# The ending of a fused vision-tower kernel in another order: last residual inside block 30's MLP product, block 29's tiles fed from the weight bank

## The chip, the core and the metric

The kernel runs on one core of one Trainium2 chip. A core has five engines that run their own instruction streams in order and wait for each other through semaphores: TensorE (PE, matrix products into PSUM), VectorE (DVE), ScalarE (ACT), GpSimd (POOL) and SyncE (SP, which here only issues transfers). ACT and POOL issue transfers too. The metric is the device time of one execution in microseconds (us); less is better. The time before is 2111.08 us, the median of three runs (2110.65 to 2120.14).

## The reference

Three stages with float32 throughout, on 16384 tokens of 256 features, in 32 blocks of 512 tokens.

```python
h = tokenizer(x)                       # windowed rfft, then @ W.T
# layer: normalised input, retention, MLP
x0 = layernorm(h)
z  = layernorm(x0) * g1 + b1
q, k, v = z @ Wq.T + bq, z @ Wk.T + bk, z @ Wv.T + bv
mem_t = decay * mem_{t-1} + k_t * v_t  # a scan along the tokens
x1 = x0 + q * mem                      # "residual" of the retention
h  = h + x1 + relu(layernorm(x1) @ W1.T + b1) @ W2.T + b2
# mixture of experts: 8 experts, the 2 best of each token
tok = layernorm(h)
p = softmax(tok @ router_w.T); two best, their shares rescaled to sum to 1
h = h + tok + sum over both of share_e * (gelu(tok @ w1[e] + b1[e]) @ w2[e] + b2[e])
```

## The kernel before

**Blocks.** `vit_tower_kernel` works through blocks 0 to 31 of 512 tokens as a software pipeline. In pass i of its loop (i = 0 to 30) block i, called `new`, is embedded and gets its retention; block i - 1, `mid`, gets its MLP (`mlp_in`, eight products of 128 hidden features each into one of three PSUM tiles called sums, then `mlp_out` in two halves u = 0, 1 of two times eight products); block i - 2, `old`, gets its choice of experts (`logits`, `choose`), the places of its rows (`place`) and its scatter. After the loop comes a hand-written ending (lines 1287 to 1371) for `last` = block 31, `mid` = block 30 and `old` = block 29.

**Tiles of tokens.** A block's tokens are scattered by expert into a buffer in HBM (`xbuf`): eight indirect writes from POOL's queue (`scatter`, line 819), two for each quarter of the block. Whenever enough are there, `take` (lines 858 to 934) makes a table on DVE that says for each new tile of 256 rows which expert it belongs to and where its rows start, and appends the tiles to a list. There are 131 such tiles, 0 to 130 in order; `take(30)` appends four that belong to block 29, `take(31)` eighteen that belong to block 30. Block 31 isn't scattered: its tokens go through all eight experts (`Expert`), with shares from `combine`.

**Steps of a tile.** `advance` runs each stage of the tiles in order, and `expert_halves` (or `expert_step`, the same in one piece) puts one step together. With n the next tile to enter, a step emits:

- *load* of the tiles up to n + 3: from SP's queue the expert's weights (641.5 KB, line 965), the rows transposed into xh (a DMA transpose, line 972) and the rows' shares and numbers into xg (line 975),
- *turn* of tile n + 1: two ACT copies that put xh's halves together into xT (line 995),
- *enter* of tile n: eight PE products into a PSUM tile of pool mm, which has two buffers (line 1002), and two Gelu activations on ACT (line 1010),
- then, in the second half, *leave* of tile n - 1: eight products into pool tm, which has three buffers (line 1019); *sums* of that tile: DVE scales them into y (lines 1031 to 1038), and POOL adds them to the output in HBM with two indirect adding transfers (line 1048); and *fetch* of the tiles up to n + 3.

A tile's two adds wait until the two adds of the tile before have landed, and for the store of the tile's block (`before = added[-2:] + [self.block.stored]`, line 1046), since they read and write the same output rows. y has four buffers, the weights w five, xh six.

**The weight bank.** The embedding's weights and inputs give up their memory once block 31 is embedded, and `load_bank` (line 938) then loads all eight experts' weights into one tile, one 641.5 KB transfer from ACT's queue per `next(weights)`. Tiles of block 30 load no weights of their own: `fetch` (line 982) copies them from the bank, on DVE or ACT by turns (line 989).

**Order.** `manual_schedule` keeps SP's, PE's, DVE's and ACT's instructions in the order in which the program emits them. So the order of the calls in the ending is the order on every engine. POOL's instructions, too, run in one order. `slot_halves` (line 1158) lets the loop run a tile step only while more than `LEFT` = 3 tiles are left.

**The ending.** Block 31 is embedded and a tile step runs; block 30's eight `mlp_in` products follow, with a tile step after the fourth and `last.features1` (eight PE transposes of zz through pool mm, copied to hT by ACT) after the sixth; then block 29's choice, a tile step and its scatter; `retention(0)`, `mlp_out(0)`, `take(30)`, `mlp_out(1)`, `retention(1)`; five tile steps with block 30's `features3` (the same for tok), choice and scatter and block 31's `residual` (transposes of ret on PE, then adds, statistics and normalisation to zz on DVE) among them; `take(31)`; block 31's `features2`, a tile step, `sum_up`, its eight `mlp_in` products with tile steps, and `mlp_out` with tile steps. Last come block 31's choice, and its eight experts among the 12 tiles that are left.

In `choose`, the weight of a token's second expert needs exp. For blocks 0 to 30 POOL raises e to that power (line 769); for block 31 ACT does it (line 767).

Of the kernel before, what the change touches and what calls it, by code (L numbers as in the profile page):

```python
# [36 lines left out]
def vit_tower_kernel(  # L37
# [312 lines left out]
    class Block:  # L350
# [381 lines left out]
        def choose(self):  # L732

            ps = self.lg
            shape = [P, TT, E]

            def wide(a):
                return a.unsqueeze(2).to_broadcast(shape)

            lg = small.tile(shape, F32, name="lg")  # L740
            top = small.tile([P, TT], F32, name="top")
            if self.i == NS:
                first_key = small.tile([P, TT], F32, name="first_key")
            else:
                first_key = self.row.bitcast(F32)[:, :, FIRST]
            turned = small.tile([P, TT, G], F32, name="turned_lg")
            nc.vector.transpose(turned.rearrange("p t g -> p (t g)"), ps.rearrange("p t g -> p (t g)"))
            nc.vector.tensor_reduce(top, turned[:, :, :E], AX.X, ALU.max)
            nc.vector.tensor_tensor(lg, turned[:, :, :E], wide(top), ALU.subtract)
            key = small.tile(shape, F32, name="key")  # L750
            self.oh = oh = small.tile([P, 2, TT, E], F32, name="oh")
            nc.vector.scalar_tensor_tensor(key, lg, 0.0, key0, ALU.is_equal, ALU.mult)
            nc.vector.tensor_reduce(first_key, key, AX.X, ALU.max)
            nc.vector.tensor_tensor(oh[:, 0], key, wide(first_key), ALU.is_equal)
            nc.vector.scalar_tensor_tensor(lg, oh[:, 0], -3.0e38, lg, ALU.mult, ALU.add)
            second = small.tile([P, TT], F32, name="second")
            nc.vector.tensor_reduce(second, lg, AX.X, ALU.max)
            nc.vector.tensor_tensor(key, lg, wide(second), ALU.is_equal)
            nc.vector.tensor_tensor(key, key, key0, ALU.mult)
            nc.vector.tensor_reduce(top, key, AX.X, ALU.max)  # L760
            nc.vector.tensor_tensor(oh[:, 1], key, wide(top), ALU.is_equal)
            dtype = F32 if self.i == NS else BF16
            self.both = small.tile(shape, dtype, name=f"both_{dtype.name}")
            nc.vector.tensor_tensor(self.both, oh[:, 0], oh[:, 1], ALU.add)
            self.ex = small.tile([P, TT], F32, name="ex")
            if self.i == NS:
                nc.scalar.activation(self.ex, second, AF.Exp)
            else:
                nc.gpsimd.tensor_tensor(self.ex, euler, second, ALU.pow)

# [7 lines left out]

        def combine(self):

            diff = small.tile([P, TT], F32, name="diff")
            second = small.tile([P, TT], F32, name="second")
            self.weights(diff, second)
            shape = [P, TT, E]
            self.share = self.both
            nc.vector.tensor_tensor(self.share, self.both, second.unsqueeze(2).to_broadcast(shape), ALU.mult)
            first = self.oh[:, 0]
            nc.vector.tensor_tensor(first, first, diff.unsqueeze(2).to_broadcast(shape), ALU.mult)
            nc.vector.tensor_tensor(self.share, self.share, first, ALU.add)
# [68 lines left out]
    def take(n, block, writes):  # L858
# [40 lines left out]
        expert = small.tile([P, KMAX], F32, name="expert")[:, :k]  # L899
        nc.vector.tensor_reduce(expert, past, AX.X, ALU.add)  # L900
        table = four.tile([P, 2, KMAX], I32, name="table")[:, :, :k]
        if block.i >= NS - 1:
            nc.vector.tensor_scalar(table[:, 0, :], expert, float(E - 1), None, ALU.min)
        else:
            nc.vector.tensor_scalar(table[:, 0, :], expert, float(P), float((E - 1) * P), ALU.mult, ALU.min)
# [47 lines left out]
    class Tile:  # L953
# [6 lines left out]
        def load(self):  # L960
            t = self.t
            self.w = five.tile([P, NW], F32, name="w")
            if self.block.i < NS - 1:
                wrow = nc.sync.value_load(self.table[:, 0, t : t + 1], min_val=0, max_val=(E - 1) * P)
                nc.sync.dma_start(out=self.w, in_=wex[bass.ds(wrow, P), :])

            def rows():
                row = nc.sync.value_load(self.table[:, 1, t : t + 1], min_val=0, max_val=ROWS - S)
                return xbuf[bass.ds(row, S), :]

            self.xh = six.tile([P, 2 * KD, S], U16, name="xh")
            read = nc.sync.dma_start(out=self.xh, in_=rows().bitcast(U16)[:, : 2 * D], transpose=True)
            unordered("rows", read, self.writes)
            self.xg = twelve.tile([P, 2, RW - D], I32, name="xg")
            read = nc.sync.dma_start(out=self.xg, in_=rows()[:, D:].rearrange("(c p) d -> p c d", p=P))
            unordered("rows", read, self.writes)
# [3 lines left out]
            return self.block.put == TT  # L980

        def fetch(self):
            if self.block.i >= NS - 1:

                assert len(loaded) == E
                t = self.t
                engine, copy = ((nc.vector, nc.vector.tensor_copy), (nc.scalar, nc.scalar.copy))[t % 2]
                e = engine.value_load(self.table[:, 0, t : t + 1], min_val=0, max_val=E - 1)
                copy(self.w.unsqueeze(1), bank[0][:, bass.ds(e, 1), :])
# [165 lines left out]

    LEFT = 3

    def slot_halves(known, load=True, sums=True):

        if len(tiles) - at["enter"] > LEFT and at["enter"] + 2 <= known:  # L1160
            yield from expert_halves(load=load, sums=sums)

    def slot(known, load=True):
# [8 lines left out]
    with tc.manual_schedule(engines=MANUAL):  # L1172
# [3 lines left out]
        for i in range(NS):  # L1176
# [54 lines left out]
            if i:  # L1231
                qkv = new.qkv()
                if old:
                    old.logits()
                    old.choose()
                if i >= EARLY:
                    next(ahead)
                next(qkv)
                next(qkv)
                tile_steps = slot_halves(known, sums=False)  # L1240
                next(tile_steps, None)
                next(qkv)
                if old:
                    writes = old.place(at_once=False)
                    old.scatter(1)
                run(tile_steps)
                if old:
                    old.scatter(2, last_product[0])
                next(qkv)
                advance("sums", at["leave"])  # L1250
                later = slot_halves(known, load=False)
                next(later, None)
                next(qkv)
                new.first_norm()
                for m in range(KD):
                    new.scan(m)
                if EARLY <= i < NB - 2:
                    xs[i + 2] = load_x(i + 2)
                mid.mlp_out(0)
                if old:  # L1260
                    old.scatter(3, last_product[0])
            else:
                xs[i + 2] = load_x(i + 2)
                new.first_norm()
                for m in range(KD):
                    new.retention(m)
# [33 lines left out]
        old.join3(nc.vector.tensor_copy)  # L1300
        for m in range(KH):
            mid.mlp_in(m)
            if m in (1, 3, 5, 7):
                next(weights)
            if m == TT - 1:
                expert_step()
            if m == KH - 3:
                last.features1()
        next(weights)
        old.logits()  # L1310
        old.choose()
        expert_step()
        writes = old.place()
        next(weights)
        restore_weights()
        last.first_norm()
        last.retention(0)
        mid.mlp_out(0)
        next(weights)
        take(NS - 1, old, writes)  # L1320
        next(weights)
        mid.mlp_out(1)
        last.retention(1)
        beside = expert_halves(fetch=False)
        next(beside)
        mid.features3()
        mid.rows()
        advance("leave", at["enter"] - 1)
        mid.logits()
        mid.choose()  # L1330
        run(beside)
        expert_step(fetch=False, sums=False)
        writes = mid.place()
        advance("sums", at["leave"])
        expert_step(fetch=False, sums=False)
        last.residual()
        expert_step(fetch=False, sums=False)
        advance("sums", at["leave"])
        expert_step(fetch=False)
        take(NS, mid, writes)  # L1340

        last.features2()
        expert_step(turn=False)
        mid.store()
        last.sum_up()
        for m in range(KH):
            last.mlp_in(m)
            if m == TT - 1:
                advance("turn", at["enter"] + 1)
            if m == KH - 3:  # L1350
                expert_step()
        expert_step()
        last.mlp_out(0, expert_step)
# [107 lines left out]
```

## Time and profile before

| what | us |
|---|---|
| median of three runs | 2111.08 |
| profiled execution | 2116.49 |
| its span, first to last instruction | 2114.7 |
| PE busy | 2077.4 (98%) |
| DVE busy | 1674.8 (79%) |
| ACT busy | 1100.8 (52%) |
| POOL busy | 886.9 (42%) |
| mean granted clock of PE | 0.994 |
| block 30's first `mlp_in` product starts | 1865.10 |
| block 31's residual, transposes start | 1925.04 |
| block 31's first `mlp_in` product starts | 1948.66 |
| block 31's choice: Exp's table load starts | 2007.14 |
| PE's last group of products | 2106.37, for 3.62 |

All starts are counted from the beginning of the span of the profiled execution. In a line of a timeline the columns are the start, the duration of the group, the engine, the line of the kernel, the operation, output and inputs with their shapes, how many, and in brackets the idle time of the engine before it and what ended that. "ACTq" and "SPq" are those engines issuing a transfer. In a line of the windows view come the stretch, its length, then for PE, PE's weight loads, DVE, ACT and POOL the busy time and the number of instructions, the granted clock, the share of the DMA engines' time, and GB/s.

### The profile page before, as it was taken

The page shows a single profiled execution, that of the slowest core. Times are in us where ns is not written, and L with a number is a line of the kernel's source. Part 1 is how long each engine was busy: PE and PEld are TensorE (multiplying, and loading weights), DVE is VectorE, ACT ScalarE, POOL GpSimd, SP SyncE. Part 2 cuts the span into 40 slices and gives each one's busy share as a digit, 9 for nine tenths or more (in the row PEclk, how much of TensorE's full clock was granted, in tenths as well). Part 3 has the DMA queues.
Part 4 walks back from the last instruction along what each step waited for, and adds up shares of the span by engine and source line. Part 5 has one row for each costly group of instructions (what it writes and reads, how often), then busy time and mean ns, then how long its engine had stood idle before and what let it go on. Part 6 is the DMA issues. An engine that isn't in the chain of part 4 may idle for free.

```text
span 2114.7 us, 30454 instructions
## 1 busy us (share of the span) xinstructions
PE 2077.4 (98%) x9042; PEld 1576.0 (75%) x9042; DVE 1674.8 (79%) x5179; ACT 1100.8 (52%) x1966; POOL 886.9 (42%) x768
## 2 busy tenths in 40 slices
PE   8999999999999999999999999999999999998999
PEld 5777677777777777777777777787777787676776
DVE  6778888888888888888888888888888888767445
ACT  2344455655545565554556555455665545543453
POOL 1032234444444444544444444444444444535444
PEclk9999999999999999999999999999999999999999
DMA  4031256766676676567667766766776567688653
GB/s 142 4 123 64 80 131 138 160 143 129 134 157 146 155 160 139 125 143 159 156 143 160 150 122 136 157 156 143 163 157 118 138 149 161 138 197 168 91 69 50
DMA packets 424519, 283.21 MB, mean 134 GB/s; under 512 B 355104, under 2 KB 391072, under 8 KB 420256
## 3 DMA queue, kind: packets, MB, share of 16 engines
q1 hardware_dynamic: 373424, 208.35, 42.5%
q0 software_dynamic: 49632, 67.39, 17.8%
q10 hardware_dynamic: 1296, 5.52, 0.8%
q8 instruction: 71, 1.16, 0.2%
q14 instruction: 96, 0.79, 0.1%
HBM read 118.36 MB, written 86.52 MB: 97 GB/s over the span
## 4 chain that ended last, share of the span: by engine, by line
PE 74%; DVE 11%; ACT 5%; DMA 5%; issue 2%; POOL 2%; SPq 1%; another core or an unknown queue 0%; ACTq 0%; DVEq 0%; POOLq 0%
PE tm L650 17%; PE sums L339 13%; PE tm L396 9%; PE sums L524 9%; PE mm L1002 8%; PE tm L1019 8%; DMA turned<-planes 3%; DVE st L263 2%; PE mm L540 1%; ACT planes L318 1%; ACT tokT L332 1%; PE tm L1098 1%; PE mm L1081 1%; PE mm L539 1%; SPq L326 1%
## 5 line engine op out<-in xcount | busy, mean ns | idle before, releaser
L1048 POOL DMA_INDIRECT out<-y,xg x226 | 369.2, 1634 | 432.7 <-DVE y L1038 220.2
L650 PE MATMUL tm<-w_sb,aT 128*128 128x256 f32 x2048 | 454.7, 380 | 0.0
L339 PE MATMUL sums<-hT,w_sb 128*128 128x512 f32 x1024 | 451.7, 593 | 1.3 <-ACT aT L640 1.3
L650 PEld LDWEIGHTS tm<-w_sb,aT 128*128 128x128 f32 x2048 | 386.7, 190 | 57.2 <-DVE z L611 4.8
L819 POOL DMA_INDIRECT xbuf<-row,to x248 | 257.1, 1037 | 294.3 <-DVE ks L560 170.5
L339 PEld LDWEIGHTS sums<-hT,w_sb 128*128 128x128 f32 x1024 | 193.4, 190 | 219.9 <-issue 201.0
L396 PE MATMUL tm<-wu,xv 128*128 128x256 f32 x1280 | 282.5, 379 | 0.0
L318 ACT COPY planes<-zz 128x1024 uint16<-128x1024 uint16 x100 | 99.3, 1041 | 342.0 <-DVE zz L292 342.0
L396 PEld LDWEIGHTS tm<-wu,xv 128*128 128x128 f32 x1280 | 242.7, 190 | 32.7
L1002 PE MATMUL mm<-xT,w 128*128 128x256 f32 x1048 | 252.5, 384 | 6.9 <-ACT xT L995 3.8
L1019 PE MATMUL tm<-w,ge 128*128 128x256 f32 x1048 | 253.4, 385 | 0.0
L1002 PEld LDWEIGHTS mm<-xT,w 128*128 128x128 f32 x1048 | 201.3, 193 | 49.9 <-issue 16.0
L1019 PEld LDWEIGHTS tm<-w,ge 128*128 128x128 f32 x1048 | 195.9, 191 | 31.4 <-issue 2.9
L640 ACT ACTIVATE aT<-sums,vec 128x512 f32<-128x512 f32 x256 | 167.0, 690 | 60.6 <-PE sums L339 59.3
L995 ACT COPY xT<-xh 128x512 uint16<-128x512 uint16 x262 | 182.1, 767 | 24.4 <-DMA xh<-xbuf 15.4
L283 POOL TENSOR_SCALAR rstd<-mv 128x4 f32<-128x4 f32 x62 | 42.0, 678 | 333.2 <-DVE mv L264 296.7
L1010 ACT ACTIVATE ge<-mm,w 128x256 f32<-128x256 f32 x262 | 109.9, 474 | 137.5 <-PE mm L1002 76.3
L1036 DVE TENSOR_TENSOR y<-tm,w 128x512 f32<-128x512 f32 x131 | 90.6, 691 | 97.9 <-PE tm L1019 86.6
L332 ACT COPY hT<-turned 128x512 uint16<-128x512 uint16 x100 | 66.2, 762 | 80.5 <-DMA turned<-planes 80.5
L263 DVE BATCH_NORM_STATS2 st<-h 128x6 f32<-128x256 f32 x256 | 104.8, 409 | 3.3
L332 ACT COPY tokT<-turned 128x512 uint16<-128x512 uint16 x116 | 76.5, 760 | 58.7 <-DMA turned<-row 58.7
L524 PE MATMUL sums<-hT,wqkv_sb 128*128 128x256 f32 x360 | 107.1, 379 | 0.0
(224 smaller groups left out, 3105.4 us busy)
## 6 DMA issues: line engine op xcount, KB each, us to landing
w<-in_wex SPq DMA_DIRECT2D x113, 641.5 KB
xb<-in_x SPq DMA_DIRECT2D x32, 1040.0 KB
out<-h SPq DMA_DIRECT2D x31, 512.0 KB
bank<-in_wex ACTq DMA_DIRECT2D x8, 641.5 KB
xbuf<-row,to POOLq DMA_INDIRECT x248
out<-y,xg POOLq DMA_INDIRECT x226
xh<-xbuf SPq DMA_TRANSPOSE x131
xg<-xbuf SPq DMA_DIRECT2D x131, 4.0 KB
```

Of the source, the lines that this page charges most:

```text
L263: nc.vector.bn_stats(self.st[:, t, :], src[:, t, :])
L332: copy(to[:, 1 - i], self.turned[:, :, i, k, :])
L339: nc.tensor.matmul(ps, lhsT=w[:, k, ts(m, P)], rhs=rhs[:, k, :], start=k == 0, stop=k == KD - 1)
L396: nc.tensor.matmul(ps[:, n, :], lhsT=xv[:, i, j, :], rhs=wu[:, i, j, :], start=j == 0, stop=j == J - 1)
L524: nc.tensor.matmul(g[:, n, :], lhsT=lhsT, rhs=rhs, start=False, stop=True, skip_group_check=True)
L640: nc.scalar.activation(self.aT[:, m, :], ps, AF.Relu, bias=vec[:, MB1 + m : MB1 + m + 1])
L650: last_product[0] = nc.tensor.matmul(ps[:, i, :], lhsT=self.aT[:, k, ts(u * 2 + i, P)], rhs=w2_sb[:, k, :], start=k == 0, stop=k == KH - 1,)
L819: write = nc.gpsimd.indirect_dma_start(out=xbuf, out_offset=bass.IndirectOffsetOnAxis(ap=self.to[:, c, t : t + 1], axis=0), in_=self.row[: ...
L995: nc.scalar.copy(halves[:, :, :, 1 - i], self.xh[:, i * KD : (i + 1) * KD, :])
L1002: nc.tensor.matmul(ps[:, m, :], lhsT=self.w[:, k * D + m * P : k * D + (m + 1) * P], rhs=self.xT[:, k, :], start=k == 0, stop=k == KD - 1,)
L1019: last_product[0] = nc.tensor.matmul(ps[:, c, :], lhsT=self.ge[:, k, ts(c, P)], rhs=w[:, (2 + k) * D : (3 + k) * D], start=k == 0, stop=k ...
L1048: add = nc.gpsimd.indirect_dma_start(out=out, out_offset=bass.IndirectOffsetOnAxis(ap=number[:, c, :], axis=0), in_=y[:, c, :], in_offset= ...
```

## The change

- The loop lets one tile more enter in pass 30 (`left=LEFT - (i == NS - 1)`), so the ending starts with one tile fewer.
- `load_bank` is driven once after each of block 30's eight products, and no longer later.
- The tile step between block 29's choice and its places is gone; `retention(0)` stands before `place`.
- `retention(1)` stands between the two products of block 30's `mlp_out(0)`, and block 31's `residual` between those of `mlp_out(1)`.
- `take(30)` stands between the two halves u = 0 and u = 1 as before; a tile step and block 31's `features2` follow `mlp_out(1)`.
- Block 31's first `mlp_in` products stand among block 30's `features3`, choice and `place`. Block 30's scatter is split into two parts with a tile step between.
- The tiles of block 29 load no weights; `fetch` copies them from the bank, as for block 30.
- In all, the ending runs one tile step fewer before `take(31)`, 13 tiles instead of 12 are left for the last stretch with block 31's experts, and the loop has run the tile between.
- Block 31's Exp moves from `choose` to `combine`, two tile steps later.

```diff
             if self.i == NS:
-                nc.scalar.activation(self.ex, second, AF.Exp)
+                self.second = second
...
         def combine(self):
 
+            nc.scalar.activation(self.ex, self.second, AF.Exp)
...
-        if block.i >= NS - 1:
+        if block.i >= NS - 2:
             nc.vector.tensor_scalar(table[:, 0, :], expert, float(E - 1), None, ALU.min)
...
-            if self.block.i < NS - 1:
+            if self.block.i < NS - 2:
                 wrow = nc.sync.value_load(self.table[:, 0, t : t + 1], min_val=0, max_val=(E - 1) * P)
                 nc.sync.dma_start(out=self.w, in_=wex[bass.ds(wrow, P), :])
...
         def fetch(self):
-            if self.block.i >= NS - 1:
+            if self.block.i >= NS - 2:
...
-    def slot_halves(known, load=True, sums=True):
-
-        if len(tiles) - at["enter"] > LEFT and at["enter"] + 2 <= known:
+    def slot_halves(known, load=True, sums=True, left=LEFT):
+
+        if len(tiles) - at["enter"] > left and at["enter"] + 2 <= known:
...
-                later = slot_halves(known, load=False)
+                later = slot_halves(known, load=False, left=LEFT - (i == NS - 1))
...
         for m in range(KH):
             mid.mlp_in(m)
-            if m in (1, 3, 5, 7):
+            if m in (0, 1, 2, 3, 4, 5, 6, 7):
                 next(weights)
             if m == TT - 1:
                 expert_step()
             if m == KH - 3:
                 last.features1()
-        next(weights)
         old.logits()
         old.choose()
-        expert_step()
-        writes = old.place()
-        next(weights)
         restore_weights()
         last.first_norm()
         last.retention(0)
-        mid.mlp_out(0)
-        next(weights)
+        writes = old.place()
+        out_steps = mid.mlp_out_steps(0)
+        next(out_steps)
+        last.retention(1)
+        run(out_steps)
         take(NS - 1, old, writes)
-        next(weights)
-        mid.mlp_out(1)
-        last.retention(1)
-        beside = expert_halves(fetch=False)
+        out_steps = mid.mlp_out_steps(1)
+        next(out_steps)
+        last.residual()
+        run(out_steps)
+        expert_step()
+        last.features2()
+        beside = expert_halves()
         next(beside)
+        last.mlp_in(0)
         mid.features3()
         mid.rows()
-        advance("leave", at["enter"] - 1)
+        run(beside)
         mid.logits()
         mid.choose()
-        run(beside)
-        expert_step(fetch=False, sums=False)
-        writes = mid.place()
-        advance("sums", at["leave"])
-        expert_step(fetch=False, sums=False)
-        last.residual()
-        expert_step(fetch=False, sums=False)
-        advance("sums", at["leave"])
-        expert_step(fetch=False)
+        expert_step()
+        writes = mid.place(at_once=False)
+        mid.scatter(2)
+        last.mlp_in(1)
+        expert_step()
+        mid.scatter(TT)
         take(NS, mid, writes)
-
-        last.features2()
-        expert_step(turn=False)
-        mid.store()
-        last.sum_up()
-        for m in range(KH):
+        for m in range(2, KH):
             last.mlp_in(m)
             if m == TT - 1:
+                expert_step(turn=False)
+                mid.store()
+                last.sum_up()
+            if m == KH - 2:
                 advance("turn", at["enter"] + 1)
-            if m == KH - 3:
+            if m == KH - 1:
                 expert_step()
         expert_step()
```

## The prediction

> **What bounds the kernel now.** I read the page first, then the windows, then PE's timeline for its gaps, and last the timelines of POOL, ACT and SP for what runs beside it.
>
> ```profile
> PE 2077.4 (98%) x9042; PEld 1576.0 (75%) x9042; DVE 1674.8 (79%) x5179; ACT 1100.8 (52%) x1966; POOL 886.9 (42%) x768
> ...
> 1865.00:1899.80 34.80, 34.80 (x138) 21.95 (x137) 19.42 (x63) 17.00 (x32) 12.58 (x9) 1.00 1.06 259
> 1899.80:1926.80 27.00, 25.24 (x126) 19.18 (x125) 21.26 (x89) 10.00 (x17) 14.34 (x14) 1.00 0.56 136
> 1926.80:1948.80 22.00, 15.51 (x60) 12.40 (x58) 16.65 (x71) 8.09 (x16) 13.69 (x12) 0.77 1.05 209
> ...
> 2000.40:2015.00 14.60, 10.54 (x58) 8.28 (x57) 9.17 (x35) 8.61 (x14) 7.72 (x6) 0.88 0.47 59
> ```
>
> PE is full everywhere but in two stretches of the ending, around the last residual (1926 to 1949) and the last choice of experts (2000 to 2015), where the granted clock falls too. PE's timeline has the gaps:
>
> ```profile
> 1938.69 1.11 PE L305 MATMUL mm<-ident,zz 128*128 128x128 f32 x4 [3.36 <-issue]
> 1942.23 3.78 PE L1002 MATMUL mm<-xT,w 128*128 128x256 f32 x8 [2.43 <-ACT hT L306]
> 1945.81 3.01 PE L1019 MATMUL tm<-w,ge 128*128 128x256 f32 x8
> ...
> 2009.97 3.44 PE L1002 MATMUL mm<-xT,w 128*128 128x256 f32 x8 [3.76 <-ACT xT L995]
> ```
>
> With 1.04, 0.72, 0.70 and 0.24 us elsewhere from 1865 on, PE idles 12.25 us. Eight products that take 1.89 us at full clock take 3.78, 3.01 and 3.44 after the long gaps, and four transposes 1.11 for 0.60: 5.1 us more. So 17.3 us is all that PE can win. The second gap is the table load for Exp (ACT 2007.14, 1.28 us, L767, then Gelu's, 2009.94, 1.28 us), with the next tile's xT queued behind it.
>
> But PE isn't alone. POOL's timeline of the scatter-adds, two per tile:
>
> ```profile
> 1952.68 1.76 POOL L1048 DMA_INDIRECT out<-y,xg  x1 [3.44 <-DVE w L989]
> 1959.77 1.54 POOL L1048 DMA_INDIRECT out<-y,xg  x1 [3.48 <-DMA out<-y,xg]
> ...
> 2099.55 1.55 POOL L1048 DMA_INDIRECT out<-y,known  x1 [2.99 <-DMA out<-y,known]
> 2101.41 1.54 POOL L1048 DMA_INDIRECT out<-y,known  x1 [0.30 <-issue]
> 2105.96 1.56 POOL L1048 DMA_INDIRECT out<-y,known  x1 [3.01 <-DVE zz L1106]
> 2107.83 1.78 POOL L1048 DMA_INDIRECT out<-y,known  x1 [0.30 <-issue]
> ```
>
> A tile's adds wait until the previous tile's have landed (L1046). The last tile's y is ready at 2101.03 (DVE L1038, 2100.41 + 0.62), yet its first add goes at 2105.96, 6.41 after the first of the pair before it. From tile 106 (1945.84) on every pair starts 6.3 to 7.5 us after the one before, though its y had been ready 3.4 to 17 us: this chain never waits for PE. From tile 108 (1959.77) to 130 it takes 146.2 us for 22 tiles, 6.645 each. PE's last product ends at 2109.99, and what follows (DVE, the store) ends the span at 2114.7; the last add, issued by 2109.61 and landed some 2.2 us later (a 6.4 us interval less 3.45 of issue and 0.8 of restart), is about 2 us ahead of that. Shorten PE alone, and after 2 us the adds set the end.
>
> The profiled execution took 2116.49 us, its span 2114.7. The median is 5.4 below. Between 1936 and 1942 DVE pauses 1.60, 1.30 and 0.77 us between instructions that wait for nothing else, and nowhere else in the trace; tile 106's adds come 8.71 after tile 105's, 2.1 over the usual interval. I take this pause as this execution's own.
>
> **The change, part by part.**
>
> *One tile more in block 30's loop.* 3.45 us of PE (L1002 and L1019, 1.73 each between starts) go before block 31's embedding; they also cover the 0.29 us wait at 1845.28. Everything behind comes 3.16 later, and one step fewer remains. Sum zero, gain 0.3.
>
> *Bank loads after each product; no tile step after the choice.* ACT issues eight 641.5 KB loads at 0.33 to 0.38 us each, inside products of 1.72 us; the issue time is hidden by PE's three sums buffers. Their waits may not be:
>
> ```profile
> 1874.10 1.06 SPq L972 DMA_TRANSPOSE xh<-xbuf  x1
> ...
> 1882.52 0.33 ACTq L944 DMA_DIRECT2D bank<-in_wex  x1
> 1882.89 1.07 ACT L306 COPY hT<-mm 128x512 f32<-128x512 f32 x2 [3.15 <-DMA xh<-xbuf]
> ```
>
> The third load stood until 1882.5 for tile 105's transposed read, issued by SP at 1874.10, 8.4 us earlier, and held the copies behind it. In the new order tile 105's *turn* itself comes into the step at m = 3, since the loop is one tile ahead. SP's chain before that read (planes, rows, store) is only 1.4 us later, so it lands at 1883.9; ACT then needs 1.38 (turn) and 0.84 (Gelu of tile 104) before PE's second features1 transposes may have their PSUM buffer: 1886.15. PE is there at 1882.4. Wait 3.75 us. Lower bound: the quickest read on the chain of waits took 6.39 (1815.45), which leaves 1.7. Upper: two more bank loads ahead, 1.9 each at the 333 GB/s of that stretch: 7.6. After it, the two gaps of 3.36 and 3.76 gave slow products and the one of 2.96 (1824.04) did not, so I add 1.55 (3.44 - 1.89): s = 5.3, between 1.7 and 9.2. [...]
>
> *Retention(1) between the halves of mlp_out(0), residual between those of mlp_out(1).* Call X the end of mlp_out(0), 1899.74 before. Now X = 1899.74 + 3.16 - 3.45 (the step gone) + 5.15 (L339 at 1906.49 to 1911.64) + s = 1904.6 + s = 1909.9. From X, DVE does 1.8 (adds and statistics, L657 to 1901.60), 3.8 (the table, to 1905.37) and 7.5 (residual, 1926.88 to 1934.37): zz at X + 13.1. PE has 3.45 + 0.87 + 3.45 + 3.45 = 11.2. It waits 1.9, and 0.4 for the first hT copy. That is the old 7.5 us wait with fillers, though not filled.
>
> *mlp_in(0) as filler.* DVE's second half of mlp_out(1) (1906.69 to 1912.80, 6.1) gives tok at X + 19.2; PE, with a tile's L1002 and one product, is there at X + 17.5: 1.7 idle.
>
> *place after one step.* DVE now has tile 104's sums (1.7), tile 105's (y after its product, to X + 23.0), the bank copy that replaces a load (0.83 and 0.86 ahead of it, 1951.06) and the choice (2.95): X + 27.7. PE comes at X + 25.5: 2.2 idle. The four weight loads saved are 2.6 MB that nothing waits for; four copies (0.83 DVE, 1.26 ACT) lie beside PE.
>
> *Exp in combine.* 2.8 us on ACT stay, but PE then has an expert's 3.43 us and a tile's 1.73 with filled buffers; I count 0.1, at most 2.8 were that cover gone. The 3.76 and 1.55 go.
>
> PE's sum: 17.6 out, 5.3 + 2.3 + 1.7 + 2.2 + 0.1 = 11.6 in, so 6.0 less. **The adds' sum decides**: tile 104's y comes behind all that DVE work, at X + 21.0 (X + 19.3 + 1.7). Tiles 105 and 106 follow at 6.65 each. Then four row scatters (1.27 each, L819) stand before tile 107's adds and four before tile 108's, each adding 2.4 to an interval (3.45 + 0.3 + 5.1 + 0.2 = 9.0): tile 108 at X + 52.3. Before, tile 104 went at 1922.93 and eight scatters held 105 until 1937.13; tile 108 at 1959.77, or 1957.7 without the pause. Now it is 1956.9 + s = 1962.2. From there the same 22 intervals and the same end run: 4.5 us later than an undisturbed before, 2.4 later than the profiled one. PE's end is over 5 us ahead of that and buys nothing.
>
> Against its own time: 2116.49 + 2.4 - 1.9 (the 2 us by which the adds were not last) = 2117.0. Against the median, which I take as without the pause, 2111.1 + 4.5 = 2115.6. I say 2115. With s at its bounds 2112 and 2119.5. The 22 intervals ranged from 6.34 to 7.47; at 6.38 throughout they save 5.8, at 6.9 they cost 5.6.
> [...]
>
> **Rivals.** (1) *PE still sets the end.* With four loads gone the intervals shrink to 6.38 and the read lands early (s = 1.7): 2115 - 5.8 - 3.6 = 2105.6, and PE's saving of 6 to 11 shows. For: the median and PE's end lay within 2 us. Against: the lag of up to 17 us. Below 2100.5 only if PE also loses its three small waits.
> (2) *ACT stands at a bank load; slower.* The eighth load issued 12.5 us after the seventh (1889.45, 1901.95), when ACT had nothing to do. Now first_norm and ks stand behind it, and PE's retention(1) needs that ks. ACT would issue it at 1891.1 and needs 3.1 after; PE comes at 1900: a wait w costs w - 5.8. At 12.5 that is 6.7: 2121.7. It decides from 12.4. Against: the loads are earlier than the reads that it stood for.
> (3) *Exp's gap only moves.* Up to 2.8 on PE, nothing on the adds: 2115.
>
> **How the numbers follow.** About 0.5% (10.6 us: 2100.5 and 2121.6) can be told from no change. My case 0.55 (2108 to 2121), rival 1 0.22 (2098 to 2108; 0.06 below 2100.5), rival 2 0.15 (2121 to 2130; 0.13 above), rival 3 and the rest 0.08 (0.01 faster, 0.02 slower). Faster 0.07, same 0.78, slower 0.15; range 2102 to 2126.
>
> **What would show it.** PE without the 3.76 us gap at the last choice, and no Exp on ACT there; a new gap of 2 to 7 us before features1's second transposes (L305 from zz) with ACT's xT waiting for xh; gaps near 2 before the last residual's and the tokens' transposes and before L796. Pairs of adds 6.3 to 7.1 apart to the last, which now lags its y by over 8 us, not 4.9; the span's last waits are for adds. I am wrong if the adds' intervals lie under 6.2 or adds wait for y.

## The result, and the profile after

The changed kernel takes 2129.36 us (median of six runs, 2123.84 to 2131.96), the kernel before 2110.86 in the runs beside it: a ratio of 1.0077, with a 95% interval of 1.0054 to 1.0101, so slower by 16 us (the two medians alone lie 18.5 us apart). I had forecast 2115, with a range from 2102 to 2126, and "slower" at 0.15. The profiled execution took 2129.20 us, its span 2127.4.

The page and the windows view of the changed kernel, in the stretches shown of before:

```profile
PE 2078.0 (98%) x9042; PEld 1576.9 (74%) x9042; DVE 1677.8 (79%) x5181; ACT 1102.0 (52%) x1968; POOL 888.3 (42%) x768
...
1865.00:1899.80 34.80, 29.48 (x103) 16.06 (x101) 12.48 (x39) 11.84 (x22) 11.52 (x8) 0.95 1.13 209
1899.80:1926.80 27.00, 19.52 (x70) 13.61 (x70) 15.50 (x53) 4.60 (x8) 8.29 (x8) 0.81 0.63 161
1926.80:1948.80 22.00, 19.04 (x90) 13.61 (x90) 18.35 (x74) 10.95 (x18) 5.50 (x4) 0.92 0.39 64
2000.40:2015.00 14.60, 14.30 (x81) 11.70 (x80) 12.86 (x50) 9.31 (x16) 6.32 (x4) 1.00 0.78 110
```

PE did as much work as before. The two stretches where it idled before are fuller now (19.04 of 22 us, 14.30 of 14.60), and the two that stand first, nearly full before (34.80 of 34.80 us, 25.24 of 27), have holes of 5.3 and 7.5 us. PE's timeline has them:

```profile
1881.20 0.66 PE L305 MATMUL mm<-ident,zz 128*128 128x128 f32 x4 [1.85 <-ACT ge L1011]
1889.34 6.96 PE L339 MATMUL sums<-hT,wqkv_sb 128*128 128x512 f32 x12 [3.47 <-ACT aT L640]
1907.36 8.18 PE L339 MATMUL sums<-hT,wqkv_sb 128*128 128x512 f32 x12 [7.48 <-ACT ks L474]
1915.38 7.07 PE L650 MATMUL tm<-w_sb,aT 128*128 128x256 f32 x32
1931.27 1.73 PE L305 MATMUL mm<-ident,zz 128*128 128x128 f32 x8 [1.04 <-DVE zz L292]
...
2109.12 3.62 PE L1099 MATMUL tm<-bank,ret 128*128 128x256 f32 x16
```

The largest, 7.48 us, stands ahead of the second retention, which waits for ks from ACT. ACT's timeline says why ks was late (ACTq lines are bank loads that it issues):

```profile
1888.21 0.33 ACTq L945 DMA_DIRECT2D bank<-in_wex  x1
1888.60 0.69 ACT L640 ACTIVATE aT<-sums,vec 128x512 f32<-128x512 f32 x1 [0.81 <-DMA bank<-in_wex]
1904.23 0.34 ACTq L945 DMA_DIRECT2D bank<-in_wex  x1
1904.67 2.07 ACT L438 ACTIVATE z<-h,shift,rstd 128x256 f32<-128x256 f32 x4 [15.38 <-DMA xh<-xbuf]
1906.64 0.67 ACT L474 ACTIVATE ks<-sums,vec 128x512 f32<-128x512 f32 x1
```

ACT had nothing to do from 1889.29 on but the eighth bank load, and that was issued at 1904.23. The first norm and ks, two short jobs, stood behind it. The bracket names a transfer into xh. It is tile 107's transposed read, in SP's timeline:

```profile
1882.60 5.42 SPq L973 DMA_TRANSPOSE xh<-xbuf  x1
```

In this trace the transfers that SP and ACT issue carry eight semaphores (100 to 105, 108 and 109; ACT's are on six of them, each of which has transfers of SP too). For 154 of these transfers the trace has the landing of the one before on the same semaphore: none of the 154 was issued ahead of it. Five of the eight bank loads went 0.02 us behind the last landing on theirs (1876.15, 1878.67, 1885.10, 1888.21 and 1904.23). The last of the five is the eighth load: it carries the same semaphore (103) as this read, whose last part had landed at 1904.21. This is the second rival of the prediction.

In the kernel before, tile 107's read went among the bank loads too, and the eighth load stood for the transfer that SP issued next (the tile's rows of shares, on semaphore 103 too; its 256 packets of 16 bytes were done at 1901.28, and the load went at 1901.95), but behind ks and not ahead of it. SP's timeline and ACT's:

```profile
1883.90 1.95 SPq L972 DMA_TRANSPOSE xh<-xbuf  x1
1886.91 0.46 SPq L975 DMA_DIRECT2D xg<-xbuf  x1
```
```profile
1889.95 0.67 ACT L474 ACTIVATE ks<-sums,vec 128x512 f32<-128x512 f32 x1
1901.95 0.33 ACTq L944 DMA_DIRECT2D bank<-in_wex  x1
```

The end, in POOL's timeline of the adds, and the last steps of the chain of waits:

```profile
1939.71 1.62 POOL L1049 DMA_INDIRECT out<-y,xg  x1 [15.34 <-DVE tile_share L1032]
...
1972.28 2.01 POOL L1049 DMA_INDIRECT out<-y,xg  x1 [0.61 <-DVE y L1039]
...
2113.66 1.76 POOL L1049 DMA_INDIRECT out<-y,known  x1 [2.96 <-DVE zz L1107]
2115.72 1.55 POOL L1049 DMA_INDIRECT out<-y,known  x1 [0.30 <-issue]
2120.27 1.57 POOL L1049 DMA_INDIRECT out<-y,known  x1 [3.00 <-DMA out<-y,known]
```
```profile
2105.82 6.94 PE tm L1099 x32
2113.66 1.76 POOL out L1049
2115.72 3.78 DMA out<-y,known
2121.84 1.86 POOLq L1457
```

Tile 104's first add goes at 1939.71, tile 108's at 1972.28, the last tile's at 2120.27: from tile 108 on, 22 intervals of 6.73 us. That last tile's y was ready at 2103.85, so its add lags it by 16.4 us, where it was 4.9 before. PE's last product ends at 2112.74, 14.7 us before the span does. Before, the chain of waits ended in PE's products; now it ends in adds that wait for adds.

### The profile page after: what moved, and what is told of

The parts are those of the page before. It is cut to its first block, busy times and chain, and to the rows that moved or that the text cites. A ratio compares the mean times of both kernels' runs of the same rounds, so it can differ in the third digit from the quotient of the medians.

```text
span 2127.4 us, 30442 instructions
## 1 busy us (share of the span) xinstructions
PE 2078.0 (98%) x9042; PEld 1576.9 (74%) x9042; DVE 1677.8 (79%) x5181; ACT 1102.0 (52%) x1968; POOL 888.3 (42%) x768
## 5 line engine op out<-in xcount | busy, mean ns | idle before, releaser
L371 DVE TENSOR_TENSOR xv<-xb 128x512 f32<-128x512 f32 x160 | 104.2, 684 | 3.2 <-DMA xb<-in_x 3.2
```

## The experiments

They were timed in four batches, each in turn with the kernel before on one chip, and each batch on another chip. That kernel's own median was 2114.8 to 2117.4 in these batches, not 2110.9, so ratios are compared, and a difference in us is the ratio's against 2110.86. The change itself was not timed again in them, so its distance from its variants is that of two ratios. The expectations' absolute times were written with 2111 for the kernel before.

| kernel | ratio to before | 95% interval | us |
|---|---|---|---|
| the change | 1.0077 | 1.0054 to 1.0101 | +16.3 |
| change, eighth load later | 1.0029 | 1.0011 to 1.0047 | +6.1 |
| change, eighth load cut to 2 KB | 1.0061 | 1.0041 to 1.0081 | +12.9 |
| change, two tiles not added | 1.0017 | 1.0002 to 1.0031 | +3.6 |
| change, weights by SP | 1.0074 | 1.0054 to 1.0095 | +15.6 |
| change, late load, two steps early | 0.9997 | 0.9984 to 1.0009 | -0.6 |
| the same, tile 106's product early too | 1.0003 | 0.9994 to 1.0012 | +0.6 |
| before, Exp alone | 0.9998 | 0.9989 to 1.0007 | -0.4 |
| before, Exp, two tiles not added | 0.9973 | 0.9962 to 0.9983 | -5.7 |
| before, two tiles not added | 0.9999 | 0.9990 to 1.0007 | -0.2 |
| before, Exp, scatters spread | 0.9984 | 0.9975 to 0.9992 | -3.4 |
| the same, two steps early | 0.9957 | 0.9941 to 0.9972 | -9.1 |
| the same, tile 106's sums early too | 0.9968 | 0.9953 to 0.9983 | -6.8 |

**Is it the eighth load?** It is taken out of the way of the norm, nothing else:

```diff
-            if m in (0, 1, 2, 3, 4, 5, 6, 7):
+            if m < KH - 1:
                 next(weights)
...
         last.retention(1)
+        next(weights)
         run(out_steps)
```

> The changed kernel, with the eighth bank load issued after the second retention instead of after the last product of block 30's first MLP matrix. Theory (the load stood 15.4 us on ScalarE and held the first norm and ks behind it): PE's wait of 7.48 us before the second retention goes, its twelve products take 6.96 us again and not 8.18, X falls by 8 to 9 us, tile 104's first add from 1939.7 to about 1931 and the end by as much: about 2121 us (2119 to 2123). Rival (the 18 us come from the adds themselves, or from the transfers of this stretch): tile 108's add stays near 1972 and the time between 2127 and 2131.

Measured 2121.46 us, 10.2 us less than the change by the ratios. PE's timeline has the second retention without a wait and at full clock (its twelve products took 5.31 us, and the granted clock was 1.00 from 1899 to 1908), and ACT's has the load standing still (until 1909.89), with nothing urgent behind it:

```profile
1897.29 3.70 PE L650 MATMUL tm<-w_sb,aT 128*128 128x256 f32 x16
1900.83 5.31 PE L339 MATMUL sums<-hT,wqkv_sb 128*128 128x512 f32 x12
1905.98 7.07 PE L650 MATMUL tm<-w_sb,aT 128*128 128x256 f32 x32
```
```profile
1891.83 2.06 ACT L438 ACTIVATE z<-h,shift,rstd 128x256 f32<-128x256 f32 x4
...
1909.89 0.34 ACTq L945 DMA_DIRECT2D bank<-in_wex  x1
1910.32 1.40 ACT L996 COPY xT<-xh 128x512 uint16<-128x512 uint16 x2 [6.89 <-DMA xh<-xbuf]
```

Tile 104's first add came at 1930.19, 9.5 us earlier, tile 108's at 1963.44, the last at 2113.59. So the wait cost some 10 of the 16 us, and it came through the adds as the theory had it. The 6.1 us that remain are near the 4.5 that my sum had against an undisturbed kernel before.

**What does the load stand for?** The load is cut, so that four columns come first:

```diff
-            nc.scalar.dma_start(out=bank[0][:, e, :], in_=wex[ts(e, P), :])
+            n = 4 if e == E - 1 else NW
+            nc.scalar.dma_start(out=bank[0][:, e, :n], in_=wex[ts(e, P), :n])
+            if n < NW:
+                yield
+                nc.scalar.dma_start(out=bank[0][:, e, n:], in_=wex[ts(e, P), n:])
...
         last.retention(1)
+        next(weights)
         run(out_steps)
```

> The changed kernel with the eighth bank load cut in two: at its place after the last product it brings four of the 1283 columns (2 KB), and the other 1279 come after the second retention. Theory (the load stands for the completion semaphore that tile 107's transposed read, issued by SyncE at 1882.6, still holds until 1904.2, and its own size is nothing to it): the small load stands 8 to 18 us all the same, PE's second retention waits 2 to 8 us, and the time is 2122 to 2131 us. Rival (ScalarE's queue takes no more data until the loads ahead have gone): four columns pass at once, the wait of the first norm is under 2 us, and the time is that of the late load, 2121 us or less.

Measured 2131.28 us; the ratio's interval holds much of that of the change. ACT's timeline:

```profile
1889.72 0.69 ACT L640 ACTIVATE aT<-sums,vec 128x512 f32<-128x512 f32 x1 [1.14 <-PE tm L723]
1904.82 0.34 ACTq L946 DMA_DIRECT2D bank<-in_wex  x1
1905.25 2.07 ACT L438 ACTIVATE z<-h,shift,rstd 128x256 f32<-128x256 f32 x4 [14.85 <-DMA xh<-xbuf]
```

2 KB stood 14.85 us, so the wait is not one for moving the load's own bytes. The first norm behind the load reads nothing of xh, and yet its bracket names the transfer into xh as what ended the wait, as in the changed kernel (15.38 us there), where the trace has the landing on the load's semaphore 0.02 us ahead of it. In two more kernels the load went at 1898.06 and 1907.52, and the first norm behind it has the same bracket (8.03 and 17.76 us).

**Do the adds set the end of the changed kernel?** The adds of two tiles are left out:

```diff
+            if self.block.i == NS - 1 and self.t in (8, 12):
+                return
             before = added[-2:] + [self.block.stored]
```

> The changed kernel without the scatter-adds of two of block 30's tiles (the ninth and the thirteenth; their products and sums stay, their rows are missing in the output). Theory (the adds set the end, 6.73 us a tile): the last add comes 13.4 us earlier, and PE's last product, which ended 14.7 us before the end of the span, then stands next to it: about 2117 us (2115 to 2120). Rival (the adds run beside something else that ends last): 2128 to 2130.

Measured 2119.21 us, 12.7 us less than the change by the ratios, with ACT's wait (17.76 us) and PE's gaps still there. PE's last product ended at 2113.76 and the span 4.9 us later: the adds set the end until PE does.

**And of the kernel before?** Exp alone is moved there, then two tiles are left out as well, then two tiles without Exp's move. The edits are those shown already.

> The kernel before, with Exp alone moved from the last choice to combine. Theory (the scatter-adds set the end within 2 us): PE's gap of 3.76 us at the last choice goes and PE's last product ends about 5.3 us earlier, but the last add does not move; 2109 to 2111 us. Rival (PE sets the end): the whole 3.76 + 1.55 us show, 2105.5 us.

Measured 2114.63 us beside 2114.91: no difference. In the profile of this kernel PE's last product ends 11 us earlier than in that of before, and the last adds come 1.8 us later, in PE's and POOL's timelines:

```profile
2095.44 3.62 PE L1099 MATMUL tm<-bank,ret 128*128 128x256 f32 x16
```
```profile
2107.76 1.56 POOL L1049 DMA_INDIRECT out<-y,known  x1 [2.98 <-DMA out<-y,known]
2109.63 1.55 POOL L1049 DMA_INDIRECT out<-y,known  x1 [0.30 <-issue]
```

> The kernel before with Exp in combine, and without the scatter-adds of two of block 30's tiles (the ninth and the thirteenth; their rows are missing in the output). With Exp alone the time did not move although PE's last product came at 2099.1 instead of 2110.0. Theory (the adds hold the end): without 13 us of adds PE sets it, 2105.6 us, about 9 less than with Exp alone (2104 to 2109). Rival (something else follows PE's end, as the sums or the stores): 2112 to 2115.

Measured 2110.42 us, 5.7 us less than before by the ratio, about what Exp's gap is worth (3.76 + 1.55). The profile has PE's last product ending at 2105.03, the last add issued by 2101.05: PE sets the end. My 2105.6 came from the early end of PE in the execution with Exp alone (2099.06), where the last residual cost less (one gap of 2.40 us and eight products of 3.66; here gaps of 3.18 and 3.31 and eight products of 3.78 and eight of 2.64), so that row was not typical.

> The kernel before without the scatter-adds of two of block 30's tiles (the ninth and the thirteenth; their rows are missing in the output), Exp where it was. Theory (in the kernel before the adds are ahead of PE's own end by about 2 us only): 1 to 4 us less than the kernel before. Rival (PE alone sets its end): no difference. Rival (the adds are far behind PE in most executions): 8 us or more less.

Measured 2117.73 us beside 2117.39, no difference. In its POOL timeline the adds behind the two left out have caught up with PE, and several wait for y only:

```profile
2077.69 1.55 POOL L1050 DMA_INDIRECT out<-y,known  x1 [7.81 <-DVE known L1043]
...
2106.32 1.54 POOL L1050 DMA_INDIRECT out<-y,known  x1 [2.80 <-DMA out<-y,known]
```

The last pair's y was ready at 2104.95, PE's last product ended at 2113.92, and the span 4.7 us after that, as in the kernel before. So there PE alone gives the time, with the adds just inside it: my 1 to 4 us were too many. Each of the two ends hides a gain in the other.

**Can the chain of adds start earlier?** In the kernel before with Exp moved, block 30's eight scatters go between the adds, and in the next kernel two tile steps are taken from the last MLP to the stretch at 1890 to 1904:

```diff
-        writes = mid.place()
+        writes = mid.place(at_once=False)
+        mid.scatter(1)
         advance("sums", at["leave"])
+        mid.scatter(2)
...
-        advance("sums", at["leave"])
+        advance("sums", at["leave"] - 1)
+        mid.scatter(3)
+        advance("sums", at["leave"])
+        mid.scatter(TT)
```
```diff
         last.retention(0)
+        expert_step()
         mid.mlp_out(0)
         next(weights)
         take(NS - 1, old, writes)
+        expert_step(fetch=False)
...
-            if m == TT - 1:
+            if m == KH - 1:
                 advance("turn", at["enter"] + 1)
-            if m == KH - 3:
-                expert_step()
-        expert_step()
         last.mlp_out(0, expert_step)
```

> The kernel before with Exp moved to combine and, besides, the eight row scatters of block 30 issued two at a time between the tiles' adds instead of all at once before tile 105's. Theory (the adds are the second limit): tile 105's adds no longer stand behind eight scatters, tile 108's first add comes at 1950 to 1953 and not at 1959.8, so PE sets the end and the gain of Exp shows: 2105.5 us (2104 to 2108). If the adds do not matter, this is the same time as with Exp alone.

> The kernel before with Exp in combine, block 30's scatters two at a time between the adds, and two tile steps earlier, one after the first retention and one after block 29's tiles are known, with two less within and behind the last MLP's first products. Theory (PE ended at 2093.3 in the run without the two early steps, 16 us ahead of the last add): tile 106's first add comes about 10 us earlier, the chain of adds ends near PE, about 2102 us (2099 to 2107). Rival (the early steps delay the last residual, and PE then waits for it): 2110 to 2116.

The scatters gave 3.4 us, not 5.5: tile 108's add came at 1954.10, and the adds still ended last (2103.79, PE at 2093.33). The steps gave 5.7 more, 2106.96 us beside 2116.85: less than both kernels, the best of this study. In its POOL timeline tile 104's adds go right behind block 29's scatters, and the last pair at 2097.94:

```profile
1906.20 1.59 POOL L1049 DMA_INDIRECT out<-y,xg  x1 [0.30 <-DVE upto L913]
1908.11 1.55 POOL L1049 DMA_INDIRECT out<-y,xg  x1 [0.30 <-issue]
1913.90 1.54 POOL L1049 DMA_INDIRECT out<-y,xg  x1 [4.24 <-DVE st L275]
...
2097.94 1.56 POOL L1049 DMA_INDIRECT out<-y,known  x1 [3.12 <-DVE h L1113]
```

PE ended at 2095.5, 9.7 us before the span, so the adds are still the limit. A third try put tile 106's products and sums ahead of `mid.mlp_out(1)` (`advance("leave", at["enter"])` and `advance("sums", at["leave"])` there):

> The kernel before with Exp in combine, scatters two at a time and two steps early, as in the run that took 2107.0, and besides with tile 106's products and sums ahead of block 30's last MLP product and not behind it. Theory (in that run tile 106's y came 12.7 us after tile 105's adds and held the chain): tile 106's first add at about 1920 and not 1926.6, the adds end some 5 us earlier, near PE's end, 2102 us (2100 to 2106). Rival (the chain only waits at its later breaks): 2106 to 2108.

Measured 2111.97 us, ratio 0.9968: no better. Tile 106's adds came at 1925.64, 8.0 us after tile 105's, but tile 107's y was ready only at 1933.51, and with three scatters ahead of it its add went at 1936.63; the break had only moved on by one tile.

**The same in the changed kernel.** The late load, and two steps early:

```diff
         old.choose()
+        expert_step()
         restore_weights()
...
         take(NS - 1, old, writes)
+        expert_step()
...
-                expert_step(turn=False)
                 mid.store()
...
-            if m == KH - 2:
-                advance("turn", at["enter"] + 1)
-            if m == KH - 1:
-                expert_step()
```

> The changed kernel with the eighth bank load behind the second retention and two of the ending's tile steps done earlier: one after the choice of block 29's experts, one after block 29's tiles are known, and none within the last MLP's first products from the third on. Theory (the adds set the end, and their chain has 40 us without an add between tiles 103 and 104): tiles 104 and 105 are added in that stretch; each step costs X 3.45 us and saves the chain 6.65; tile 106's first add at about 1937, the end near 2110 us (2107 to 2116). Rival (what counts is PE's order, not where the chain of adds begins): 2121 us, as with the late load alone.

Measured 2117.44 us, 0.6 us under the kernel before by the ratio. The mechanism holds, 6.7 us came, but not the 11 hoped for. POOL's timeline has two breaks:

```profile
1889.55 1.56 POOL L1049 DMA_INDIRECT out<-y,xg  x1 [0.30 <-issue]
...
1909.63 1.63 POOL L1049 DMA_INDIRECT out<-y,xg  x1 [14.72 <-DMA out<-y,xg]
...
1940.93 1.54 POOL L1049 DMA_INDIRECT out<-y,xg  x1 [13.54 <-DVE y L1039]
```

Tile 104's adds had y at 1896.86 and stood until tile 103's, issued by 1891.1, had landed: some 18 us, among the bank loads. Tile 106 then waited for y. The next kernel put its products between the halves of `mlp_out(1)`, ahead of the last residual:

> The changed kernel with the late load and the two early steps of the run that took 2117.4, and besides with tile 106's second products and sums between the halves of the second MLP product, ahead of the last residual, and not behind it. Theory (in that run the chain of adds waited 17 us for tile 106's y, and ended the span; PE's last product came at 2107.3, 9 us ahead of the span's end): tile 106's first add at about 1930 and not 1940.9, and PE sets the end, 4.7 us after its last product: 2113 us (2110 to 2116), a little under the kernel before. Rival (the adds lose the gain again at the scatters and in the stretch of the bank copies): 2117 to 2119.

Measured 2116.23 us, ratio 1.0003: no gain. Tile 106's add did come at 1932.94, but tile 104's stood 18.4 us behind its y (12.8 in the kernel before this one), and tiles 107, 110, 113 and 114 waited for their y. The adds ended the span again (2106.97; PE at 2104.77).

**Are the bank copies to blame?** Block 29's tiles load weights through SP again (three lines back to `NS - 1`):

> The changed kernel with block 29's tiles loading their weights from HBM through SyncE again, and not copying them from the bank. Theory (the four copies lie beside PE and the adds, the four loads wait for nothing): no difference to the changed kernel, 2127 to 2131 us. Rival one (the copies on VectorE and ScalarE delay the sums and so the adds): 2121 to 2126. Rival two (the saved 2.6 MB shorten the adds' intervals): 2132 to 2136.

Measured 2130.92 us (2122.27 to 2137.87); the ratio is that of the change. The copies cost nothing that shows within its interval of about 4 us either way. Its profiled execution was one of the quick ones, 2122.3 us, and it is a smaller dose of the same wait, in ACT's timeline and PE's:

```profile
1888.68 0.34 ACTq L945 DMA_DIRECT2D bank<-in_wex  x1
1889.80 0.69 ACT L640 ACTIVATE aT<-sums,vec 128x512 f32<-128x512 f32 x1 [1.78 <-PE sums L339]
1898.06 0.35 ACTq L945 DMA_DIRECT2D bank<-in_wex  x1
1898.51 2.07 ACT L438 ACTIVATE z<-h,shift,rstd 128x256 f32<-128x256 f32 x4 [8.03 <-DMA xh<-xbuf]
```
```profile
1901.21 5.42 PE L339 MATMUL sums<-hT,wqkv_sb 128*128 128x512 f32 x12 [1.67 <-ACT ks L474]
```

A wait of 8.03 us on ACT costs PE 1.67, one of 15.38 costs 7.48 and slow products, and with the load behind the retention it costs PE nothing. Two of the four kernels with this load ahead of the norm also scatter the widest of all: 2117.17 to 2140.58 with the cut load, 2122.27 to 2137.87 here.

## Why the prediction was wrong, point by point

- **The adds decide the end.** Right. In the changed kernel leaving out two tiles' adds gave 12.7 us, and in the kernel before PE's gain from Exp alone gave nothing. That the adds stood 2 us inside PE's end there was about right: leaving some out gave nothing.
- **From X on.** Nearly right. Tile 104's add came 20.8 us after X (X is the end of `mlp_out(0)`, 1918.9; I had 21.0), tile 108's 53.4 (52.3), and the 22 intervals took 148.0 (146.2). POOL ran six scatters ahead of tile 107's adds and two ahead of tile 108's, not four and four; the intervals were 11.87 and 6.66, and their sum was off by 0.5.
- **X itself: the step that failed.** I had X at 1909.9, with nothing in the sum for ACT standing at the eighth bank load. It came 9.0 us later: 7.48 of wait and 2.76 of slow products (8.18 for twelve that take 5.42 where the wait was short) make 10.2, and the rest of X came 1.2 early. With the load moved X was 1909.5. My second rival had the mechanism word for word, and I gave it 0.15. Its case against itself, "the loads are earlier than the reads that it stood for", was wrong: tile 107's read hardly moved. SP issued it at 1883.90 in the kernel before, and it landed at 1901.71; in the changed one at 1882.60, 6.7 us before ACT came to the eighth load, and it landed at 1904.21. The load stood in both kernels, from 1890.62 to 1901.95 before. What the new order changed is the work behind it: none that PE waited for then, the first norm and ks now. I also priced the rival at the old wait of 12.5 us with 5.8 covered; it was 15.38 with 7.9 covered, and the slow products came on top.
- **The sum's base.** I took 2116.49 to be an odd execution, for DVE's pauses near 1940, and went by the median of three, 2115 and not 2117. That was not safe. DVE pauses at the same place in two more profiled kernels with this part of the old order (0.89, 2.01 and 0.80 us in the one before with two tiles not added), though not in the one with Exp alone, and the kernel before ran at 2114.8 to 2117.4 in the later batches. From the sum against its own time, 2117.0, the three misses (9.0, 1.1 and 1.8) lead to 2128.9; 2129.20 was profiled.
- **PE's sum.** Right in the total, by luck in part. From the first product behind the loop's last Gelu gap (L539, 1824.04 before) to the last product PE took 285.95 us before and 279.52 with the late load: 6.4 less, where I had 6.0. In that kernel the wait at `features1` was 3.54 us with 1.55 of slow products (I had 3.75 and 1.55), in the changed kernel 1.85 with none. A wait for aT at `retention(0)`, 1.02 us there and 3.47, with 1.54 of slow products, in the changed kernel, was not in my list; in the changed kernel ACT had stood until 1885.10 at the fifth bank load, for SP's weight load of 1877.00 on its semaphore (105), which landed at 1885.08, so it is the same kind of wait. Of the rest, in the changed kernel, `features2` had 1.04 and 0.24 (I had 1.9 and 0.4), `place` 1.68 (2.2), the wait of 1.7 for tok did not come, and Exp's gap is gone.
- **Bank copies and SP's four loads.** Right, as far as the interval goes: no effect shows.
- **Rival 1, PE sets the end.** It holds for the kernel before, and in it only for as long as PE gains nothing.

## What to carry to other kernels

A transfer that an engine issues is an instruction in its queue, and it can stand for the landing of another engine's transfer, as ACT's eighth load did for SP's read (ACT idle for 15.38 us, the load issued 0.02 us behind the landing): before you put one ahead of urgent work, look up in the trace which earlier transfer it has to see landed, and issue it behind that work. A wait that costs nothing where it stands, as ACT's 11 us before, becomes a cost once other work is put behind it. And when two chains end within 2 us of each other, price the second one first: a gain in the first is worth nothing until the second is started earlier (with Exp alone PE's last product came 11 us earlier, and the time moved by 0.4).

## What the runs showed of the hardware

- **One slow read holds up many.** Tile 107's read took 21.6 us from issue to landing, and 17.8 in the kernel before; the median of the changed kernel's reads is 5.1. ACT stood idle for 15.38 us behind it, with the eighth load, the first norm and ks in its queue, and PE waited 7.48 for that ks. Windows of the changed kernel, with the DMA engines' busy share and GB/s in the last two columns:

```profile
1872.00:1884.00 12.00, 10.15 (x39) 6.35 (x38) 4.40 (x13) 3.34 (x6) 3.54 (x3) 1.00 1.08 339
1884.00:1902.00 18.00, 12.41 (x50) 6.54 (x48) 3.06 (x14) 3.00 (x5) 4.05 (x3) 0.91 1.32 112
```

  In the second stretch the DMA engines counted as busier and moved a third as much, with two transposed reads issued among the bank loads (1882.60 and 1892.65, whose issue alone took 5.42 and 5.23 us against a median of 1.26 for the 131 of this kernel). No run here has these reads without the loads, so which of the two is slowed by the other, and why, stays open.
- **The clock after a gap.** The first four transposes after an idle time of 3.26 us took 0.66 us in one kernel and 1.12 in another (the two with early steps in the changed order), on the same instruction. PE's timelines of the two:

```profile
1885.46 0.66 PE L305 MATMUL mm<-ident,zz 128*128 128x128 f32 x4 [3.26 <-ACT ge L1011]
```
```profile
1882.38 1.12 PE L305 MATMUL mm<-ident,zz 128*128 128x128 f32 x4 [3.26 <-ACT ge L1011]
```

  Both lost the same, at different places: in the first the eight products behind the transposes took 5.29 us for 3.60, in the second 4.80 for 3.60 on top of the transposes' 1.12 for 0.60, some 1.7 us in each. The granted clock from 1878 to 1884 was 1.00 in the first and 0.86 in the second. The clock records of the kernel before and the changed one, up to PE's last product, have the clock halved in eight stretches, which last 3.41 us (five), 6.83 (one) or 10.24 (two). There is no sharp bound in these runs: PE was slow behind a gap of 2.64 us in the kernel with the late load (two products, L539, took 1.04 for 0.70), and not behind one of 2.95 in the changed kernel (0.70). So my rule that 3.36 slows and 2.96 doesn't was wrong, in its reading too: behind the gap of 2.96 in the kernel before the clock was halved from 1825.19 on, for 3.41 us, and eight products (L1002, 1826.53) took 2.92 us for 1.89.
- **An adding transfer among bulk loads** can be late: tile 103's second add landed 20.7 us after its issue had ended in the changed kernel, where those of the last three tiles took 2.0 to 2.3. In the two with early steps in the changed order tile 104's first add, which is ordered behind it, went 18.5 and 24.3 us after that issue had ended (1909.63 and 1912.13).
